# The reciprocal root of a block's variance: from GpSimd's power to Newton's steps on VectorE

## The chip, the cores and the metric

The kernel runs on one core of one Trainium2 chip. The metric is the device time of one execution in microseconds, as the median of repeated runs. The engines go by the profile's names: PE is TensorE, DVE is VectorE, ACT is ScalarE, POOL is GpSimd, SP is SyncE.

## The reference

x has 8 batches of 4096 rows by 256 values, adj is 4096 by 4096 and sparse, W is 256 by 256, all in float32. With A = relu((adj + adj^T) / 2), D the row sums of A and r = D^-0.5:

```
L   = I - diag(r) A diag(r)
out = relu(L @ (x @ W))            # for each batch
y   = (x + out - mean) / sqrt(var + 1e-5)   # over the 256 values of a row
```

The last line is what the change is about: each row of each batch needs the reciprocal square root of its variance.

## The kernel before

**First stage (up to about 600 us).** The adjacency is loaded in 512 by 512 tiles, symmetrised on TensorE and VectorE, and written to a scratch matrix a_dram. x @ W is formed, scaled by r and written to a scratch matrix g_dram, in which one row holds all 8 batches of a node (2048 values, 8 KB).

**Second stage.** The 4096 output rows are 32 blocks of 128. Block 0 is finished from products made in the first stage. The other 31 are worked off in 16 pairs u, block 2u + 1 and block 2u + 2, in the order SEQ = 1 to 7, 0, 8 to 15. For each pair an index list names the source nodes that have an entry in the pair's rows, sorted by which 64-row halves they touch. The list is cut into tiles of 128 nodes, 302 over all pairs (29 in pair 0, 24 in pair 1, 16 to 22 in the others, 9 in pair 15). A tile is one step:

- GpSimd issues two indirect DMAs: `ga` (L707), the tile's 128 rows of a_dram, and `g` (L718), its 128 rows of g_dram, up to 1 MB. The `g` tiles lie in a ring of 13 buffers. Gather n + 13 is issued in the program behind the products of tile n, whose slot it takes.
- TensorE multiplies (L905): 4 column pieces of 512 for each block that the tile touches. Products that touch only half a block (64 rows) run two at a time.

When a block has its last product, `finish` runs: ScalarE evicts four PSUM banks to `y` (`evict`, L608), VectorE adds the residual `xr` (L619) and makes the moments (L624, L626), L627 adds EPS to the variance, and `normalise` makes the power -0.5 on GpSimd (L632), subtracts the mean and multiplies on VectorE (L634, 8 instructions, one a batch), and stores the block from SyncE's queue (L642). There are four buffers for `xr`, whose loads go out on ScalarE's queue (L602), and one for `y`. The last block, 31, has a way of its own (`finish_last`): its additions and powers are on GpSimd, its scaling on ScalarE.

**The lists.** While a pair runs, VectorE and TensorE make the lists of later pairs. `prepare` puts the spreading of the list of the pair two places ahead (`spread`, L274 to L290) and the patterns of the pair four places ahead (L184 to L199) on VectorE. `lists`, after the first block of a pair is finished, puts the counting on TensorE (L209, L210, L241, L242, L295); it needs the results of L199 and L290. Its results lie in two PSUM banks that VectorE reads (L307, L308, L169 to L174), and the index steps follow (L311 to L265, L222 to L236). The gathers two pairs on read `ai` and `gi`, which come out of this.

**What sets the order.** Each engine has one queue that is worked off in order, and the code writes that order out. `queue(engine)` sets an instruction behind the last one traced on that engine. `after(n, fn)` calls a function once n further counts of products have been traced, a half block counting 1 and a whole block 2 per tile:

```
            def rest():
                z = xr.pop(i)
                with queue("dve"):
                    mv, rstd = moments(i, y, z, stat)

                def end():
                    in_turn(normalise, i, z, mv, rstd)

                after(6, end)

            after(1, rest)
```

A pair has 26 to 59 counts (10 in pair 15). GpSimd's power is part of `normalise` and so stands in GpSimd's queue between the gathers traced before and after that point; since a gather is traced 13 tiles ahead of its products, the gathers in front of a power belong to tiles up to 13 further on. A branch that computes everything densely stands at the end for inputs that the lists don't hold; it is not taken here.

Of the kernel before, what the change touches and what calls it, by code (L numbers as in the profile page):

```python
# [9 lines left out]
F32 = mybir.dt.float32  # L10
AF = mybir.ActivationFunctionType
ALU = mybir.AluOpType
AX = mybir.AxisListType
BF16 = mybir.dt.bfloat16
I32 = mybir.dt.int32
# [29 lines left out]
def kernel(  # L45
# [25 lines left out]
    nc = tc.nc  # L71
    B, N, F = x.shape
    FO = w.shape[1]
    P = 128
# [26 lines left out]
    neg_half = const.tile([P, NB], F32, name="neg_half")  # L101
# [58 lines left out]
    def blocks(u):  # L160

        return min(2, NB - 1 - 2 * u)
# [442 lines left out]
    def evict(i, py, ypool):  # L605
        y = ypool.tile([P, B, FO], F32, tag="y", name=f"y_{i}", bufs=1)
        for c in range(G // S):
            nc.scalar.activation(  # L608
                y.rearrange("p b o -> p (b o)")[:, c * S : (c + 1) * S],
                py[c],  # L610
                AF.Relu,
                scale=minus_r[:, i : i + 1],
            )
        return y

    def moments(i, y, z, stat, tag="", adder=nc.vector):

        n = z.shape[1]
        adder.tensor_add(z, z, y)  # L619
        stats = stat.tile([P, n, 6], F32, tag=f"stats{n}", name=f"stats_{i}{tag}")  # L620
        mv = stat.tile([P, n, 2], F32, tag=f"mv{n}", name=f"mv_{i}{tag}")
        rstd = stat.tile([P, n], F32, tag=f"rstd{n}", name=f"rstd_{i}{tag}")
        for b in range(n):
            nc.vector.bn_stats(stats[:, b, :], z[:, b, :])  # L624
        for b in range(n):
            nc.vector.bn_aggr(mv[:, b, :], stats[:, b, :])  # L626
        nc.vector.tensor_scalar(rstd, mv[:, :, 1], EPS, None, ALU.add)  # L627
        return mv, rstd

    def normalise(i, z, mv, rstd):  # L630
        n = z.shape[1]
        nc.gpsimd.tensor_tensor(rstd, rstd, neg_half[:, :n], ALU.pow)  # L632
        for b in range(n):
            nc.vector.tensor_scalar(  # L634
                z[:, b, :],
                z[:, b, :],
                mv[:, b, 0:1],
                rstd[:, b : b + 1],
                ALU.subtract,
                ALU.mult,  # L640
            )
        nc.sync.dma_start(out[:, i * P : (i + 1) * P, :].rearrange("b p f -> p b f"), z)  # L642
# [4 lines left out]
    def targets(u, kind):  # L647

        if kind == 0:
            kind = 15 if blocks(u) == 2 else 3  # L650
        out = []
        for b in range(2):
            h = kind >> 2 * b & 3
            if h:
                out.append((b, {1: slice(0, Q), 2: slice(Q, P), 3: slice(0, P)}[h]))
        return out
# [15 lines left out]
    with (  # L672
# [9 lines left out]
        stat = gath.enter_context(tc.tile_pool(name="stat", bufs=3))  # L682
# [10 lines left out]
        def queue(engine):  # L693

            traced = reversed(nc.cur_bb.bb.instructions)
            return tc.issue_after(next(i for i in traced if i.engine == engines[engine]))
# [34 lines left out]
        def after(n, fn, *args):  # L731
            later.append((n, fn, args))

        def run_later(by):
            ready = [l for l in later if l[0] <= by]
            later[:] = [(n - by, fn, args) for n, fn, args in later if n > by]
            for _, fn, args in ready:
                fn(*args)
# [4 lines left out]
        n = RING  # L743
# [30 lines left out]
        def finish(i):  # L774

            if i == NB - 1:
                finish_last(i)
                return
            with queue("act"):
                y = evict(i, py.pop(i), ypool)  # L780

            def rest():
                z = xr.pop(i)
                with queue("dve"):
                    mv, rstd = moments(i, y, z, stat)

                def end():
                    in_turn(normalise, i, z, mv, rstd)

                after(6, end)  # L790

            after(1, rest)

# [66 lines left out]
        def in_turn(fn, *args):  # L860

            with queue("dve"):
                fn(*args)
# [4 lines left out]
        for q, (u, step) in enumerate(steps):  # L868
            new = q == 0 or steps[q - 1][0] != u
            last = q + 1 == len(steps) or steps[q + 1][0] != u  # L870
            if new:
                after(11, prepare, u)
                after(10 if u != SEQ[-1] else 4, residuals, range(2 * u + 1, 2 * u + 1 + blocks(u)))
                left = {}
                for v, st in steps[q:]:
                    if v == u:
                        for k, t in st:
                            for b, _ in targets(u, k):
                                left[b] = left.get(b, 0) + 1
                begun = set()  # L880
                for b in range(blocks(u)):
                    py[2 * u + 1 + b] = []
            work = [(b, rows, *got[u, t]) for m in range(2) for k, t in step for b, rows in targets(u, k)[m : m + 1]]
            if work[0][1] == side != slice(0, P):
                work.reverse()
            side = work[-1][1]
            for b in sorted({wk[0] for wk in work}):
                if not py[2 * u + 1 + b]:
                    py[2 * u + 1 + b] = [
                        psum.tile([P, S], F32, tag=f"b{b}", name=f"py_{u}_{b}_{c}") for c in range(G // S)  # L890
                    ]
            fresh = []
            for b, rows, at, gt in work:
                hs = {(b, h) for h in range(2) if rows.start <= h * Q < rows.stop}
                assert not hs & begun or hs <= begun
                fresh.append(not hs & begun)
                begun |= hs
                left[b] -= 1
            for c in range(G // S):
                for (b, rows, at, gt), new_rows in zip(work, fresh):  # L900
                    both = any(len(targets(u, k)) == 2 for k, t in step)
                    off = b * P if both else 0

                    with queue("pe"):
                        last_product = nc.tensor.matmul(  # L905
                            py[2 * u + 1 + b][c][rows, :],
                            lhsT=at[:, off + rows.start : off + rows.stop],
                            rhs=gt[:, c * S : (c + 1) * S],
                            start=new_rows,
                            stop=left[b] == 0,  # L910
                            skip_group_check=True,
                        ).ins
            for k, t in step:
                gather(n)
                n += 1
            run_later(sum(1 + (rows == slice(0, P)) for _, rows, _, _ in work))
            for b in {wk[0] for wk in work}:
                if left[b] == 0:
                    finish(2 * u + 1 + b)
                    if b == 0:  # L920
                        after(2, lists, u)
# [9 lines left out]
    with tc.If(short > 0):  # L931
        with (
            tc.tile_pool(name="full", bufs=3) as full,
            tc.tile_pool(name="ypool3", bufs=2) as ypool,
            tc.tile_pool(name="stat3", bufs=3) as stat,
        ):
            for i in range(NB):
                lt = full.tile([P, NB, P], F32, tag="l", name=f"l_{i}", bufs=2)
                nc.sync.dma_start(
                    lt, a_dram[:N, i * P : (i + 1) * P].rearrange("(m p) q -> p m q", p=P)  # L940
                )
                py = [psum.tile([P, S], F32, tag="b0", name=f"pz_{i}_{c}") for c in range(G // S)]
                for m in range(NB):
                    gt = full.tile([P, G], F32, tag="g", name=f"gf_{i}_{m}", bufs=4)
                    nc.sync.dma_start(gt, g_dram[m * P : (m + 1) * P, :])
                    for c in range(G // S):
                        nc.tensor.matmul(
                            py[c],
                            lhsT=lt[:, m, :],
                            rhs=gt[:, c * S : (c + 1) * S],  # L950
                            start=(m == 0),
                            stop=(m == NB - 1),
                        )
                y = evict(i, py, ypool)
                z, _ = residual(i, ypool)
                mv, rstd = moments(i, y, z, stat)
                normalise(i, z, mv, rstd)


# [26 lines left out]
```

## Time and profile before

| | |
|---|---|
| median of 14 runs | 1627.08 us (1622.49 to 1629.72) |
| the profiled execution | 1628.85 us, span 1627.1 us |
| TensorE busy | 1496.9 us, 92% |
| VectorE busy | 828.8 us, 51% |
| GpSimd busy | 795.0 us, 49% |
| ScalarE busy | 372.5 us, 23% |
| moved by DMA | 575.69 MB, mean 354 GB/s |
| mean granted TensorE clock | 0.965 |

A line of the groups of instructions reads: line, engine, operation, what it writes <- what it reads, shapes, count | busy time in us, mean of one in ns | idle time of that engine just before these instructions and what ended most of it. A line of the waits reads: who <- for whom: us in total, how many times, the longest. A line of the timeline reads: start, length, engine, line, operation, and in brackets the idle time before it with what ended it. A line of the stretches reads: from:to, length, busy time (and instructions) of PE, PEld (weight load), DVE, ACT and POOL, the granted clock, the mean busy share of the 16 DMA engines, and GB/s. GpSimd's busy time in a gather is the making of its descriptors; the transfer comes after it.

### The profile page before, as it was taken

The numbers are of one execution on the slowest core, as the hardware profiler recorded it, in microseconds if no ns is written. First come the engines' busy times: TensorE is split into PE (matmuls) and PEld (weight loads), VectorE is DVE, ScalarE is ACT, GpSimd is POOL, SyncE is SP. The second block draws the span as 40 slices with busy tenths as digits, with TensorE's granted clock in tenths as the row PEclk, the third lists the DMA queues.
The fourth block names the chain that finished last, engine by engine and source line by source line (L and its number), as shares of the span: only waits on it lengthen the run. The fifth ranks groups of instructions, "written<-read, shape, count | busy, mean of one in ns | idle before, by whom it ended". The sixth has DMA issues, their size and how long they took to land.

```text
span 1627.1 us, 18626 instructions
## 1 busy us (share of the span) xinstructions
PE 1496.9 (92%) x6544; PEld 779.6 (48%) x6544; DVE 828.8 (51%) x1878; ACT 372.5 (23%) x462; POOL 795.0 (49%) x1120
## 2 busy tenths in 40 slices
PE   6999989998879898999999999779999899899893
PEld 5787877776666643333333333223333333333331
DVE  5675678876445604253543726445054734743543
ACT  3555554544334510101001001000001001010111
POOL 3011010101011157676777767676477777667773
PEclk9999999999989999999999999989999999999997
DMA  9999999999778889999999999899698999999995
GB/s 339 371 367 404 389 370 374 400 395 341 265 290 290 346 352 406 396 400 358 404 369 369 375 345 385 326 381 373 227 332 332 347 387 364 347 371 368 340 360 194
DMA packets 229715, 575.69 MB, mean 354 GB/s; under 512 B 20403, under 2 KB 119011, under 8 KB 191875
## 3 DMA queue, kind: packets, MB, share of 16 engines
q0 software_dynamic: 56672, 305.70, 49.0%
q1 hardware_dynamic: 100912, 134.23, 23.5%
q10 hardware_dynamic: 72032, 134.51, 22.1%
q8 instruction: 54, 0.88, 0.2%
q14 instruction: 45, 0.37, 0.1%
HBM read 479.07 MB, written 136.34 MB: 378 GB/s over the span
## 4 chain that ended last, share of the span: by engine, by line
PE 61%; DVE 13%; DMA 12%; issue 7%; POOL 4%; ACT 2%; POOLq 0%; SPq 0%; ACTq 0%; DVEq 0%; another core or an unknown queue 0%
PE py L905 40%; PE pg L457 9%; PE lead L420 5%; PE tr L360 4%; DMA a_dram<-sym 3%; PE xtr L446 3%; DMA xin<-in_x_dram 3%; DVE sym L364 2%; DMA g<-g_dram,gi 2%; DVE xr L634 2%; POOL g L718 2%; POOL ga L707 1%; DVE hot L274 1%; DMA ga<-a_dram,ai 1%; DMA adj<-in_adj_dram 1%
## 5 line engine op out<-in xcount | busy, mean ns | idle before, releaser
L905 PE MATMUL py<-g,ga 128*64 128x512 f32 (+1 forms) x3152 | 937.1, 603 | 18.4 <-issue 12.1
L905 PEld LDWEIGHTS py<-g,ga 128*64 128x64 f32 (+1 forms) x3152 | 338.1, 154 | 605.9 <-issue 583.2
L718 POOL DMA_INDIRECT g<-g_dram,gi x302 | 339.7, 1125 | 182.1 <-issue 89.5
L707 POOL DMA_INDIRECT ga<-a_dram,ai x302 | 327.5, 1084 | 98.6 <-issue 80.1
L608 ACT ACTIVATE y<-py,minus_r 128x512 f32<-128x512 f32 x120 | 82.0, 687 | 900.9 <-PE py L905 703.8
L634 DVE TENSOR_SCALAR xr<-xr,mv,rstd 128x256 f32<-128x256 f32 x248 | 86.7, 420 | 363.3 <-POOL rstd L632 316.8
L457 PE MATMUL pg<-w_sb,xt 128*128 128x256 f32 x1024 | 234.5, 388 | 5.3 <-ACT xt L447 5.2
L364 DVE TENSOR_TENSOR sym<-tr,adj 128x512 f32<-128x512 f32 x256 | 162.8, 681 | 125.9 <-PE tr L360 109.3
L457 PEld LDWEIGHTS pg<-w_sb,xt 128*128 128x128 f32 x1024 | 197.2, 195 | 34.4 <-ACT xt L447 6.0
L369 DVE TENSOR_REDUCE part<-sym 128x32 f32<-128x2048 f32 x64 | 145.3, 2277 | 63.7 <-ACT sym L368 63.7
L619 DVE TENSOR_TENSOR xr<-xr,y 128x2048 f32<-128x2048 f32 x31 | 71.2, 2296 | 190.7 <-ACT y L608 129.5
L415 POOL DMA_DIRECT2D strip<-a_dram x32 | 18.5, 581 | 294.6 <-PE lead L420 289.3
L360 PE MATMUL tr<-ident,adj 128*128 128x128 f32 x1024 | 137.6, 285 | 24.8 <-DVE sym L364 12.4
L368 ACT ACTIVATE sym<-sym 128x2048 f32<-128x2048 f32 x64 | 122.5, 1914 | 120.6 <-DVE sym L364 120.6
L360 PEld LDWEIGHTS tr<-ident,adj 128*128 128x128 f32 x1024 | 119.6, 146 | 53.0 <-DVE sym L364 24.4
L446 PE MATMUL xtr<-ident,xin 128*128 128x128 f32 x512 | 74.5, 292 | 22.8 <-DVE sym L364 13.6
L389 POOL TENSOR_TENSOR r<-e,neg_half 128x4 f32<-128x4 f32 x8 | 8.3, 1041 | 172.8 <-DVE e L388 172.8
L624 DVE BATCH_NORM_STATS2 stats<-xr 128x6 f32<-128x256 f32 x256 | 87.2, 411 | 7.2 <-POOL xr L619 6.1
L420 PE MATMUL lead<-gt,strip 128*128 128x512 f32 x176 | 82.5, 593 | 0.0
L447 ACT COPY xt<-xtr 128x512 f32<-128x512 f32 x128 | 69.0, 590 | 50.4 <-PE xtr L446 49.0
L446 PEld LDWEIGHTS xtr<-ident,xin 128*128 128x128 f32 x512 | 60.9, 149 | 39.9 <-DVE sym L364 23.8
L467 ACT ACTIVATE gt<-pg,r 128x512 f32<-128x512 f32 x88 | 60.5, 687 | 79.3 <-PE pg L457 72.0
(108 smaller groups left out, 609.6 us busy)
## 6 DMA issues: line engine op xcount, KB each, us to landing
adj<-in_adj_dram SPq DMA_DIRECT2D x64, 1024.0 KB
a_dram<-sym ACTq DMA_DIRECT2D x64, 1024.0 KB
xin<-in_x_dram SPq DMA_DIRECT2D x64, 512.0 KB
xr<-in_x_dram ACTq DMA_DIRECT2D x32, 1024.0 KB
out_dram<-xr SPq DMA_DIRECT2D x31, 1024.0 KB
g_dram<-gt ACTq DMA_DIRECT2D x22, 1024.0 KB
g_dram<-held ACTq DMA_DIRECT2D x10, 1024.0 KB
ga<-a_dram,ai POOLq DMA_INDIRECT x302
```

What stands on the lines that cost most here:

```text
L360: ins = nc.tensor.transpose(pt[:, c * P : (c + 1) * P], tji[:, c, a * P : (a + 1) * P], ident)
L364: nc.vector.tensor_add(sym[:, a, :], pt, tij[:, a, :])
L368: nc.scalar.activation(sym, sym, AF.Relu, scale=0.5)
L369: nc.vector.tensor_reduce(part[:, i * A : (i + 1) * A, j * S // Q : (j + 1) * S // Q], sym.rearrange("p a (c q) -> p a c q", q=Q), AX.X, A ...
L420: nc.tensor.matmul(lead[c], lhsT=strip, rhs=g[:, c * S : (c + 1) * S], start=not done, stop=len(done) == NB - 1, skip_group_check=True,)
L446: nc.tensor.transpose(pt[:, k, c, :], xin[b // H][:, b % H + k, c * P : (c + 1) * P], ident)
L457: ins = nc.tensor.matmul(pg[:, k * FO : (k + 1) * FO], lhsT=xt[:, b + k, c, :], rhs=w_sb[:, c, :], start=(c == 0), stop=(c == FC - 1),)
L624: nc.vector.bn_stats(stats[:, b, :], z[:, b, :])
L634: nc.vector.tensor_scalar(z[:, b, :], z[:, b, :], mv[:, b, 0:1], rstd[:, b : b + 1], ALU.subtract, ALU.mult,)
L707: nc.gpsimd.indirect_dma_start(out=at if both else at[:, :P], out_offset=None, in_=a_pairs if both else a_rows, in_offset=bass.IndirectOff ...
L718: nc.gpsimd.indirect_dma_start(out=gt, out_offset=None, in_=g_dram, in_offset=bass.IndirectOffsetOnAxis(ap=gi[:, t : t + 1], axis=0), boun ...
L905: last_product = nc.tensor.matmul(py[2 * u + 1 + b][c][rows, :], lhsT=at[:, off + rows.start : off + rows.stop], rhs=gt[:, c * S : (c + 1) ...
```

## The change

The root is made on VectorE. The bits of v = variance + EPS are taken as an integer and shifted right by one, turned into a float, and subtracted from a constant; the result, taken as float bits, is a first guess of v^-0.5. Three of Newton's steps follow. These are 12 instructions on 128 x 8 values, each needing the one before. They are called right behind `moments`, in VectorE's queue. `normalise` has no instruction on GpSimd any more and is called 3 counts later instead of 6. `prepare` is called 6 counts into a pair instead of 11. `finish_last` keeps its four powers and four additions on GpSimd, behind the last gather.

```diff
+    def inverse_root(i, v, stat):
+
+        n = v.shape[1]
+        half = stat.tile([P, n], F32, tag="half", name=f"half_{i}")
+        bits = stat.tile([P, n], I32, tag="bits", name=f"bits_{i}")
+        root = stat.tile([P, n], F32, tag="root", name=f"root_{i}")
+
+        nc.vector.tensor_single_scalar(bits, v.bitcast(I32), 1, ALU.arith_shift_right)
+        nc.vector.tensor_copy(half, bits)
+        nc.vector.tensor_scalar(root.bitcast(I32), half, -1.0, float(0x5F3759DF), ALU.mult, ALU.add)
+        for _ in range(3):
+            nc.vector.tensor_mul(half, root, root)
+            nc.vector.scalar_tensor_tensor(half, half, -0.5, v, ALU.mult, ALU.mult)
+            nc.vector.scalar_tensor_tensor(root, half, 1.5, root, ALU.add, ALU.mult)
+        return root
+
     def normalise(i, z, mv, rstd):
-        n = z.shape[1]
-        nc.gpsimd.tensor_tensor(rstd, rstd, neg_half[:, :n], ALU.pow)
-        for b in range(n):
+        for b in range(B):
...
                 with queue("dve"):
-                    mv, rstd = moments(i, y, z, stat)
+                    mv, var = moments(i, y, z, stat)
+                with queue("dve"):
+                    rstd = inverse_root(i, var, stat)
 
                 def end():
                     in_turn(normalise, i, z, mv, rstd)
 
-                after(6, end)
+                after(3, end)
...
-                after(11, prepare, u)
+                after(6, prepare, u)
...
-                mv, rstd = moments(i, y, z, stat)
-                normalise(i, z, mv, rstd)
+                mv, var = moments(i, y, z, stat)
+                normalise(i, z, mv, inverse_root(i, var, stat))
```

## The prediction

> **What bounds the kernel now.** I read the page first, then the waits of the second stage (from 581 us on, where the gathers start), then the timeline around the longest wait of TensorE, and last the stretches. On the page TensorE is busy for 1496.9 of 1627.1 us, so what can be won is small and lies in its gaps. The page's group of VectorE's normalising step shows the odd thing:
>
> ```profile
> L634 DVE TENSOR_SCALAR xr<-xr,mv,rstd 128x256 f32<-128x256 f32 x248 | 86.7, 420 | 363.3 <-POOL rstd L632 316.8
> ```
>
> VectorE stands idle for 363.3 us ahead of this line, for GpSimd's power (L632). The waits of the second stage say who pays for that:
>
> ```profile
> DVE xr L634 <- POOL rstd L632: 313.1, 28, 32.6
> PE lists L209 <- DVE kind L199: 29.8, 4, 15.1
> POOL rstd L632 <- DVE rstd L627: 20.8, 6, 5.5
> PE lists L295 <- DVE val L290: 7.2, 2, 6.1
> PE py L905 <- DMA g<-g_dram,gi: 4.9, 3, 2.5
> ```
>
> TensorE waits 29.8 + 7.2 = 37.0 us for VectorE's index lists, and only 4.9 us for a gather. The timeline of the worst case shows the chain, and how tight the gathers are beside it:
>
> ```profile
> 1002.30 0.17 DVE L627 TENSOR_SCALAR rstd<-mv 128x8 f32<-128x8 f32 x1
> ...
> 1035.08 1.02 POOL L718 DMA_INDIRECT g<-g_dram,gi  x1 [0.63 <-DMA g<-g_dram,gi]
> 1036.12 1.67 POOL L632 TENSOR_TENSOR rstd<-rstd,neg_half 128x8 f32<-128x8 f32 x1
> 1037.83 2.86 DVE L634 TENSOR_SCALAR xr<-xr,mv,rstd 128x256 f32<-128x256 f32 x8 [32.57 <-POOL rstd L632]
> ...
> 1064.11 0.47 PE L209 MATMUL lists<-kind,ones 128*128 128x352 bf16 x1 [15.07 <-DVE kind L199]
> ...
> 1065.17 1.95 POOL L718 DMA_INDIRECT g<-g_dram,gi  x1 [0.30 <-issue]
> ```
>
> The variance is ready at 1002.5. The power stands in GpSimd's queue behind gathers that are themselves late, and runs at 1036.12. VectorE waits 32.57 us, then works almost without a pause up to the lists, and TensorE, which needs them, waits 15.07 us. The stretches (us, busy time by engine, clock, DMA share, GB/s; the last two for the product tiles alone) say what lies behind that:
>
> ```profile
> 581.00:1077.00 496.00, 471.43 (x1849) 174.95 (x1849) 220.34 (x616) 38.72 (x57) 359.92 (x319) 0.99 0.98 373
> 1077.00:1195.00 118.00, 114.18 (x372) 43.07 (x370) 32.45 (x92) 6.18 (x9) 69.59 (x66) 0.97 0.85 314
> 1195.00:1590.00 395.00, 372.28 (x1432) 139.38 (x1430) 198.16 (x583) 39.86 (x59) 285.69 (x249) 0.97 0.97 358
> 640.00:740.00 100.00, 100.00 (x373) 38.46 (x373) 38.89 (x103) 6.91 (x11) 71.59 (x64) 1.00 1.02 400
> 1092.00:1102.00 10.00, 7.24 (x11) 2.27 (x12) 0.00 (x0) 0.66 1.02 400
> 1102.00:1126.00 24.00, 24.00 (x64) 9.19 (x63) 0.00 (x0) 1.00 1.03 402
> ```
>
> The DMA engines are nearly full throughout (0.97 to 0.98). Only from 1077 to 1195, where pair 0 has most products per gather, is TensorE clearly the slower side. At the end the gathers decide:
>
> ```profile
> 1589.45 1.00 POOL L718 DMA_INDIRECT g<-g_dram,gi  x1 [0.39 <-issue]
> 1595.54 5.35 PE L905 MATMUL py<-g,ga 128*64 128x512 f32 x16 [2.54 <-DMA g<-g_dram,gi]
> 1602.64 3.62 PE L905 MATMUL py<-g,ga 128*64 128x512 f32 x14 [1.75 <-DMA g<-g_dram,gi]
> ```
>
> So two chains run side by side: products with their lists, and the supply of gathers. The change touches both.
>
> **Removed.** 31 powers leave GpSimd. In the trace they cost 51.8 us of work and 21.5 us of idle queue ahead of them, 73.3 us, mostly between gathers. The 363.3 us of VectorE's idle time go with them.
>
> **Added.** 12 dependent instructions a block on 8 columns. The nearest rows are the small index steps:
>
> ```profile
> 903.28 0.17 DVE L252 SCALAR_TENSOR_TENSOR fits<-pos_r,rest 128x32 f32<-128x32 f32 x1
> ...
> 904.14 1.01 POOL L718 DMA_INDIRECT g<-g_dram,gi  x1 [0.30 <-issue]
> ...
> 904.82 0.31 DVE L265 CAST at<-digit 128x32 f32<-128x32 int32 x1
> ```
>
> L252 to L265 are eight dependent steps, and seven starts take 904.82 - 903.28 = 1.54 us, 0.22 us each. Twelve make 2.6 us a block and 82 us for 31. VectorE is busy some 467 of the 1047 us from 581 to 1628, and would be busy 549: no bound. Where GpSimd was free, the power took 1.9 us from variance to normalising, so a block's own chain gets 0.7 us longer. That is covered by the spare time below; if it were not, it would cost 31 x 0.7 = 22 us at most.
>
> **Moved.** Normalising is set 3 counts after the root instead of 6, list building (L274 to L199) 6 counts into a pair instead of 11, and in the order of the built program list building now stands ahead of the previous block's normalising. Normalising issues the store on SyncE's queue, so stores start earlier and the four residual buffers come free earlier; they add no bytes. No queue gets a new wait: the gathers keep their order on GpSimd and their waits for ring slots. What is newly queued behind the root is the reading of the lists (L307 on), which frees two PSUM banks that the next pair's products need. In pair 4 that reading starts at 875.25 after 1.93 us of waiting for TensorE, ends at 878.1, and the next pair starts at 881.8: a root of 2.6 us fills the wait, moves the end by 0.7 us and leaves 3 us to spare, so I cost it at nothing.
>
> **Where TensorE's 37.0 us go.** In the worst case the wait of 32.6 us disappears and two roots cost 5.3, so the lists come 27 us earlier against a wait of 15.1. The other three long ones (6 to 7 us, near 1294, 1417 and 1524) each follow a VectorE wait of 19.9 to 25.3 us. The earlier list building comes on top. All 37.0 should go. Slow products that follow a wait go too: in 1092 to 1102 eleven product passes ran at a clock of 0.66, which at the next stretch's 64 in 24 us are worth 4.1 us, so 6 us were lost there. All that TensorE can give back is 37.0, about 12 for such slow stretches (6 here, as much again near 1327 and right after the waits), 4.9 for gathers and 5 in the tail: 59 us.
>
> **What is late next: gathers.** Pair 0 starts at 1077, and its first gathers are issued only at 1058.45, 1062.51 and 1065.17; at the end a gather is used 11 to 13 us after its issue when TensorE waits for it. With an unchanged supply pair 0 could start only some 4 us earlier. The supply itself gains from an emptier queue, but no more than the DMA engines have left: 0.98 to 1.02 over 496 us is 19 us. I take half, 8 to 9, since part of that idle time is start-up and full ring. With the 6 us of slow clock, 4 + 9 + 6 = 19 us by 1195; the bounds are 4 and 27 (waits of 3 and 15.1, rows of slow products 9). From 1195 to 1590 the supply sets the pace. GpSimd's row for that window:
>
> ```profile
> L632 POOL TENSOR_TENSOR rstd<-rstd,neg_half 128x8 f32<-128x8 f32 x14 | 23.4, 1671 | 18.3 <-DVE rstd L627 18.0
> ```
>
> A queue that alone set the pace would give back 23.4 + 18.3 = 41.7 us. The DMA engines allow less: a share of 0.97 filled up to 1.00 gives 12 us, to 1.02 19 us. I take 15, with bounds 6 and 32, the latter being what is left of TensorE's 59. In the tail, block 30's power at 1610.03 and its normalising up to 1614.3 stand before the last block's statistics; ahead of time they free 4 us (0 to 5).
>
> **The sum.** 19 + 15 + 4 = 38 us. The profiled execution took 1628.85 us for a span of 1627.1, and lies 1.8 us above the median of 1627.08. 1628.85 - 38 = 1591, from the median 1589; I say 1590. The bounds are 11 us (1617) and 59 us (1568).
>
> **A rule that speaks against it.** GpSimd's gather at 1065.17 took 1.95 us instead of 1.00 under VectorE's large addition, while the one at 904.14 took 1.01 us in the midst of the small chain. I take the second row, no cost. The Trainium skill, SBUF — State Buffer, section Who interferes with whom, says that a VectorE instruction with two SBUF inputs contends with a GpSimd instruction that reads SBUF, and that copies and tensor_scalar in a 2-port mode block GpSimd outright. By it all 12 steps could hold up gathers, and in place of the 38 us won the sum would come near the loss of rival 3.
>
> **Rivals.**
> 1. *The DMA engines are as full as they get.* For it: shares of 0.97 to 0.98 and 20 us stretches at 1.0 with only 370 to 380 GB/s. Against it: 400 GB/s from 640 to 740. Then only 4 + 6 and a little of the tail is won: 1612 to 1617.
> 2. *TensorE sets the pace alone,* the queue was the limit: up to 59 us, 1568 to 1576. Against it: the waits for gathers at the end.
> 3. *Slower: the roots hold up the gathers.* If each root stopped descriptor making for its 2.64 us, GpSimd would lose 82 us and gain 73.3; the gathers, and with them the end, come 8.5 us later, 1636. It decides from 2.36 us a block on. The row at 904.14 speaks against it.
> 4. *No change:* lists or stores are held by something that the power's wait hid, and the end stays at 1627.
>
> **Chances.** The forecast (1577 to 1606) 0.62, rival 1 0.14, rival 2 0.12, rival 3 0.07, no change 0.05. Within 0.2% (3.3 us) is about what a measurement here cannot tell from no change. Faster 0.88, same 0.05, slower 0.07. The range 1568 to 1617 leaves out the last two cases and the edges of the first.
>
> **What would show it.** Right: no wait of VectorE at normalising, no wait of TensorE at L209 or L295 above 1 us, no clock row below 0.9 between 700 and 1500, twelve small VectorE rows near 0.2 us, gathers of 1.0 us as before, a DMA share of 1.0 from 1195 on, and more TensorE waits for gathers than 4.9 us. Wrong: gathers that take clearly longer under the roots, lists still late, or a DMA share that stays at 0.97 while the gathers are no faster.

## The result and the profile after

The changed kernel took 1608.41 us (median of 10 runs, 1600.28 to 1612.74) beside 1627.37 us for the kernel before: a ratio of 0.9889, 95% interval 0.9873 to 0.9904. In three later sets of runs it was 0.9883 (0.9855 to 0.9911), 0.9909 (0.9876 to 0.9941) and 0.9918 (0.9892 to 0.9944). So it is faster, by 11 to 20 us (the medians of each set), and not by the 37 that were forecast. The profiled execution has a span of 1610.9 us against 1627.1.

The group of VectorE's normalising step, from the page of the changed kernel (what was L634 is L648 now):

```profile
L648 DVE TENSOR_SCALAR xr<-xr,mv,root 128x256 f32<-128x256 f32 x248 | 83.9, 409 | 0.1
```

The idle time ahead of it fell from 363.3 to 0.1 us. The waits from 581 us on (L732 and L721 are the two gathers, L718 and L707 before; L921 are the products, L905 before), first two of the kernel before, then the changed kernel:

```profile
POOL g L718 <- PE py L905: 54.3, 47, 4.6
...
POOL g L718 <- DMA g<-g_dram,gi: 29.1, 30, 1.9
```

```profile
DVE xr L619 <- ACT y L608: 383.6, 19, 72.5
...
POOL g L732 <- PE py L921: 71.7, 54, 4.6
POOL g L732 <- DMA g<-g_dram,gi: 60.0, 53, 2.3
...
POOL g L732 <- DMA ga<-a_dram,ai: 25.2, 21, 2.6
...
PE py L921 <- DMA g<-g_dram,gi: 17.7, 15, 3.2
...
PEld L209 <- DVE xr L619: 2.4, 3, 0.8
```

Three things are to be seen. TensorE's waits for lists (37.0 us before) are gone; of what is left at L209 and L295 the largest is a weight load's 2.4 us. In their place stand 17.7 us of waits for gathers, all of them behind pair 0. VectorE's idle time has not gone but moved: it now waits 383.6 us for ScalarE to evict the next block (129.5 before). And GpSimd, which got rid of 73.3 us of powers and of waiting for their data, now waits longer ahead of its gathers: 60.0 us for an earlier `g` to land (29.1 before), 25.2 for an earlier `ga` (none before), 71.7 put down to products (54.3 before). That is 73.5 us more: the queue's freed time became waiting.

The list step in pair 7 on TensorE, from the timeline, where the kernel before stood still for 15.07 us; now no wait stands in front of it:

```profile
1059.84 1.88 PE L921 MATMUL py<-g,ga 128*128 128x512 f32 x4
1061.55 0.31 PE L209 MATMUL lists<-kind,ones 128*128 128x352 bf16 x1
```

And the stretches of the changed kernel, cut at the start and the end of pair 0 as they are now:

```profile
581.00:1073.00 492.00, 481.18 (x1848) 176.57 (x1848) 250.45 (x802) 39.71 (x59) 333.10 (x305) 0.99 0.98 374
1073.00:1182.00 109.00, 109.00 (x372) 41.97 (x370) 34.92 (x110) 5.18 (x9) 66.35 (x66) 1.00 0.94 347
1182.00:1580.00 398.00, 376.79 (x1432) 141.81 (x1430) 236.54 (x788) 38.60 (x58) 259.14 (x235) 0.99 0.97 362
```

The DMA share was 0.98, 0.85 and 0.97 before; it is 0.98, 0.94 and 0.97. It rose only in pair 0, where TensorE had wasted time. By the starts of products in the two traces, the 16.2 us of span split up like this:

| part | before | after | won |
|---|---|---|---|
| start of pair 0 | 1077.0 | 1073.1 | 3.9 |
| from there to the start of pair 8 | 118.8 | 109.3 | 9.5 |
| from pair 8 to the end of the last product | 410.4 | 413.7 | -3.3 |
| the tail after it | 20.9 | 14.8 | 6.1 |

Behind pair 0, in a quarter of the span and with 19.1 of TensorE's 37.0 us of list waits, nothing was won.

### The profile page after: what moved, and what is told of

The parts are those of the page before. It is cut to its first block, busy times and chain, and to the rows that moved or that the text cites. A ratio compares the mean times of both kernels' runs of the same rounds, so it can differ in the third digit from the quotient of the medians.

```text
span 1610.9 us, 18973 instructions
## 1 busy us (share of the span) xinstructions
PE 1505.6 (93%) x6544; PEld 781.8 (49%) x6544; DVE 890.7 (55%) x2250; ACT 371.9 (23%) x462; POOL 735.7 (46%) x1089
## 4 chain that ended last, share of the span: by engine, by line
PE 65%; DMA 17%; DVE 8%; issue 5%; POOL 2%; ACT 2%; SPq 0%; POOLq 0%; ACTq 0%; DVEq 0%; another core or an unknown queue 0%
PE py L921 43%; DMA g<-g_dram,gi 10%; PE pg L457 10%; PE lead L420 5%; PE tr L360 3%; PE xtr L446 3%; DVE sym L364 3%; DMA a_dram<-sym 3%; DMA xin<-in_x_dram 2%; DMA adj<-in_adj_dram 1%; DVE part L369 1%; POOL ga L721 1%; ACT sym L368 1%; DMA xr<-in_x_dram 1%; POOL g L732 1%
## 5 line engine op out<-in xcount | busy, mean ns | idle before, releaser
L921 PE MATMUL py<-g,ga 128*64 128x512 f32 (+1 forms) x3152 | 949.0, 601 | 36.0 <-DMA g<-g_dram,gi 17.7
L921 PEld LDWEIGHTS py<-g,ga 128*64 128x64 f32 (+1 forms) x3152 | 341.8, 153 | 631.7 <-issue 601.0
L732 POOL DMA_INDIRECT g<-g_dram,gi x302 | 342.0, 1132 | 248.7 <-issue 81.4
L721 POOL DMA_INDIRECT ga<-a_dram,ai x302 | 317.7, 1052 | 100.4 <-issue 84.7
L619 DVE TENSOR_TENSOR xr<-xr,y 128x2048 f32<-128x2048 f32 x31 | 71.2, 2297 | 452.9 <-ACT y L608 383.6
L446 PE MATMUL xtr<-ident,xin 128*128 128x128 f32 x512 | 73.7, 290 | 23.6 <-DVE sym L364 14.7
L648 DVE TENSOR_SCALAR xr<-xr,mv,root 128x256 f32<-128x256 f32 x248 | 83.9, 409 | 0.1
```

Source lines behind the costliest of these rows:

```text
L446: nc.tensor.transpose(pt[:, k, c, :], xin[b // H][:, b % H + k, c * P : (c + 1) * P], ident)
L648: nc.vector.tensor_scalar(z[:, b, :], z[:, b, :], mv[:, b, 0:1], rstd[:, b : b + 1], ALU.subtract, ALU.mult,)
L721: nc.gpsimd.indirect_dma_start(out=at if both else at[:, :P], out_offset=None, in_=a_pairs if both else a_rows, in_offset=bass.IndirectOff ...
L732: nc.gpsimd.indirect_dma_start(out=gt, out_offset=None, in_=g_dram, in_offset=bass.IndirectOffsetOnAxis(ap=gi[:, t : t + 1], axis=0), boun ...
L921: last_product = nc.tensor.matmul(py[2 * u + 1 + b][c][rows, :], lhsT=at[:, off + rows.start : off + rows.stop], rhs=gt[:, c * S : (c + 1) ...
```

## The experiments

The theory that the first four runs put to the test: transfers set the pace of the gathers, so only the list wait ahead of pair 0 and the tail cost time. Rival A gives the gain to the earlier list building, rival B to every list wait and every power alike. The median of the kernel before differed from one set of runs to another (1616 to 1629 us), so each kernel is read by its ratio to the runs of before beside it. "The stretch" is always the time from pair 8's first product to the end of the last product.

**The root alone.** Diff against the changed kernel:

```diff
-                after(3, end)
+                after(6, end)
...
-                after(6, prepare, u)
+                after(11, prepare, u)
```

> The root is made on VectorE as after the change, but the two delays of before stay (normalising 6 counts after the root, list building 11 counts into a pair). Theory (the DMA engines set the pace of the gathers; only the list wait ahead of pair 0 and the tail cost time): the list wait is gone already with the root alone, so about 1609 us, 1605 to 1613. Rival A (earlier list building is what wins): no more than half of the 18 us, 1617 to 1627.

Measured: 1603.46 us beside 1616.06, ratio 0.9914 (0.989 to 0.9938). That is 13 to 14 us, more than the half of the 18 that rival A allowed. The forecast in us was meant from 1627 and can't be read from 1616.

**The delays alone**, the power still on GpSimd (the same two lines of the change, made in the kernel before).

> The power stays on GpSimd as before, only the two delays of the change are made (3 counts and 6 counts). Theory: normalising still waits for GpSimd, but list building now stands ahead of the previous block's normalising and misses most of the wait: the 13 us ahead of pair 0 mostly won, the tail's 6 not, 1612 to 1620 us. Rival A as in the first run: the power is the whole cause, and normalising that is queued earlier waits longer: 1624 to 1632.

Measured: 1613.40 us, ratio 0.9979 (0.9963 to 0.9996). The time lies in the range, but that range was meant from 1627 us; beside 1616 only 3.4 us were won, not most of 13. The waits of this run from 581 us on tell more than the time:

```profile
DVE xr L634 <- POOL rstd L632: 374.1, 17, 33.0
...
PE py L905 <- DMA g<-g_dram,gi: 36.8, 21, 3.8
...
PE lists L209 <- DVE kind L199: 5.8, 2, 4.8
```

Normalising waits for GpSimd as long as ever, yet the lists hardly wait any more, since their building now stands ahead of it. TensorE got 28 of its 37.0 us of list waits back (5.8 and 3.1 are left) and waits 36.8 us for gathers. So getting rid of most of these waits was by itself worth little. The waits for gathers alone don't tell why: the root alone, in the same set, has 35.6 us of them and is 10 us faster. By the starts of products, the run with the delays alone begins pair 0 5.5 us later than the root alone, gains 3.1 in pair 0, and loses 5.1 in the stretch (415.6) and 4.6 in the tail (20.3).

**The change in one half of the pairs.** The early half:

```diff
-                with queue("dve"):
-                    rstd = inverse_root(i, var, stat)
+                if i <= 16:
+                    with queue("dve"):
+                        rstd = inverse_root(i, var, stat)
...
+                    after(3, end)
+                else:
+                    def end():
+                        in_turn(normalise_power, i, z, mv, var)
+
+                    after(6, end)
...
-                after(6, prepare, u)
+                after(6 if u <= 7 else 11, prepare, u)
```

> The change (root and delays) for the blocks up to 16 and the list building of pairs 1 to 7 and 0 alone; later blocks have the power on GpSimd and the old delays. Theory (only the list wait ahead of pair 0, and the tail, cost time; later list waits are hidden behind the gathers): 13 of the 18 us are won, 1614 us (1611 to 1617). Rival B (every list wait and every power in the queue costs): about half is won, 1618 us or more.

The late half (`i > 16`, `u > 7`):

> The reverse: root and delays of the change only from block 17 and pair 8 on; the earlier blocks as before. Theory: the tail alone is won, 4 to 6 us: 1621 to 1623 us. Rival B: half of the 18 us or more, 1618 us or less.

Measured: early 0.9955 (0.9938 to 0.9971), 7 us; late 0.996 (0.9944 to 0.9976), 6.5 us. By the ratios it looks like rival B's even split, but the traces say where the late half's share lies: its stretch takes 409.5 us and its tail 14.7, where the early half's stretch takes 413.5 and its tail 20.8. These are TensorE's waits in the stretch, first in the early half's run, whose stretch is built as before, then in the late half's:

```profile
PE lists L209 <- DVE kind L199: 23.4, 3, 13.3
...
PE lists L295 <- DVE val L290: 6.5, 1, 6.5
...
PE py L932 <- DMA g<-g_dram,gi: 4.5, 2, 2.5
```

```profile
PE py L932 <- DMA g<-g_dram,gi: 23.7, 20, 2.6
```

29.9 us of list waits went, 19 us of waits for gathers came, and the stretch is 4 us shorter, but it also began 10 us later. Beside the 410.4 us of the kernel before, the late half wins the tail and next to nothing else. The early half began pair 0 at 1062.8 instead of the 1076.1 of the late half's run, lost 3 of these 13.3 us in pair 0 and 4 more in the stretch; so the theory's 13 us were won at that place and half of them did not last.

**The whole change again, and fewer bytes.** The next runs test what holds the stretch. The changed kernel as it is:

> The changed kernel itself, beside the next three on one chip. Both theories: 0.987 to 0.991 of before. In its profile the stretch from the start of pair 8 to the last product takes 409 to 414 us, as in every profile so far, with the change or without.

Measured: 1609.01 us beside 1629.49, ratio 0.9883 (0.9855 to 0.9911); the stretch takes 414.3 us. The same with a quarter of the stores left out:

```diff
-        nc.sync.dma_start(out[:, i * P : (i + 1) * P, :].rearrange("b p f -> p b f"), z)
+        nc.sync.dma_start(out[:6, i * P : (i + 1) * P, :].rearrange("b p f -> p b f"), z[:, :6])
```

> The changed kernel that stores only 6 of the 8 batches of every block but the last (the output of two batches is left out): 8.1 MB less for the DMA engines, some 22 us of their time at 366 GB/s, half of it behind pair 0; TensorE, VectorE and GpSimd have the same work. Theory (the DMA engines set the pace behind pair 0): the time falls by 12 to 20 us against the changed kernel, 8 to 11 of them between pair 8 and the last product. Rival C (waits of gathers for one another, or TensorE, set it): 0 to 5 us.

> The same cut of the stores in the kernel before (two batches of the output left out). Theory: also limited by the DMA engines behind pair 0, so 8 to 16 us less than before; ahead of pair 0 the list wait stays and eats most of that half. Rival C': the kernel before is limited by the list waits and powers in the queue and not by transfers: 0 to 4 us.

Measured: 0.9845 (0.9816 to 0.9874) for the changed kernel, 6 us less than whole, and 0.9926 (0.9903 to 0.9949) for the kernel before, 12 us less. The stretch falls from 414.3 to 402.3 us, and in the kernel before to 406.1 from the 410.4 of its first profile. In the stretch the theory's 8 to 11 us are there, though the profile is of the fastest of the five runs; by the medians, of runs that scatter by 12 us, the changed kernel's 6 us lie near the rival's end. So a larger cut was made: 2 of 8 batches stored (`out[:2`, `z[:, :2]`).

**The changed kernel a third time, and with few stores:**

> The changed kernel once more, as the measure for the next three on one chip: 0.986 to 0.991 of before.

> The changed kernel that stores only 2 of the 8 batches of every block but the last (the output of six batches is left out): 24.4 MB less, some 67 us of the DMA engines' time, 32 of them behind pair 0. Theory (transfers set the pace behind pair 0 until TensorE does): the stretch from pair 8 to the last product falls from 413 to 384 to 392 us, which is what it holds without TensorE's waits; the time falls by 20 to 32 us. Rival C (not the bytes, but gathers waiting for one another, four in flight): no further than with 8.1 MB less, the stretch stays at 400 us or above and the time falls by 4 to 12 us.

Measured: 1611.13 us (ratio 0.9909, 0.9876 to 0.9941) and 1571.17 us (0.9673, 0.9643 to 0.9702), 40 us apart, more than expected. The stretch falls from 412.3 to 385.0 us, as the theory said, with TensorE busy 365.4 of 370:

```profile
1166.00:1536.00 370.00, 365.38 (x1428) 138.49 (x1426) 231.65 (x768) 38.21 (x57) 262.12 (x234) 0.99 0.96 357
```

What I had not counted is that the pairs ahead of pair 0 are held by transfers too: pair 0 starts at 1055.5 instead of 1072.9. Nothing on TensorE, VectorE or GpSimd was changed here; leaving out bytes gave 40 us. The share is 0.96 and the rate 357 GB/s, almost as with all stores (0.97 and 362), though TensorE now hardly waits. Shorter stores also free the residual buffers sooner; no run parts the two.

**The change with few stores.** If list waits and transfers run side by side and the later one counts, the change must be worth more once transfers are few. Both sides of it, first in different sets of runs and then side by side (the measure for the first set was the changed kernel once more):

> The changed kernel, as the measure for the next three on one chip: 0.986 to 0.992 of before.

Measured: 1605.11 us beside 1615.86, 0.9918 (0.9892 to 0.9944).

> The kernel before with stores of 2 of 8 batches for every block but the last (the output of six batches is left out), to be set against the changed kernel with the same cut (0.9673 of before). Theory (list waits and transfers run side by side, and the later one sets the time): with fewer transfers the list waits that the change removes decide, so the change is worth more, 28 to 40 us: 0.985 to 0.992 of before, with 25 us or more of list waits in the profile. Rival E (the list waits never cost anything but ahead of pair 0): the change is worth 18 us or less here too, 0.979 or below.

> The changed kernel with stores of 2 of 8 batches for every block but the last, beside the next run on one chip: 0.966 to 0.972 of before.

> The kernel before with the same cut. Theory (waits and transfers side by side, the later one counts): 22 to 34 us slower than the run beside it, more than the change is worth with all stores. Rival E (transfers have no part in what the change is worth): 10 to 20 us slower.

Measured: the kernel before with the cut 0.9814 (0.9792 to 0.9837), which is 0.0141 or 23 us off 0.9673, between the two theories; but there the kernel before took 1615.86 us and for the 0.9673 it took 1626.41, so the two are a poor pair. Side by side: 1556.12 us (0.9624, 0.9597 to 0.965, a little lower than expected) against 1584.74 us (0.9791, 0.9766 to 0.9816), 28.6 us apart by the medians and 27 by the ratios. With all stores the change is worth 11 and 13 us by the same two measures in the set whose kernel before took 1615.86 us, much like the 1617.82 here. TensorE's waits from 581 us on, of the kernel before with the cut:

```profile
PE lists L209 <- DVE kind L199: 25.0, 4, 13.0
...
PE lists L295 <- DVE val L290: 5.6, 2, 5.0
PE py L905 <- DMA g<-g_dram,gi: 2.2, 1, 2.2
```

and the one that answers to them in the changed kernel with the cut:

```profile
PE py L921 <- DMA g<-g_dram,gi: 10.6, 7, 2.6
```

Here the list waits (30.6 us) are paid for, and taking them away brings 27 to 29 us. The stretch alone falls from 398.5 to 386.1 us, where with all stores the change won nothing in it. This shows the cause: the waits were real and could be removed, but with all stores transfers take more than half of them back (11 to 13 us are left in sets of this kind). Rival E falls.

**What the queue and the small instructions cost.** GpSimd also makes the power, into a tile that nobody reads (3 counts behind the root, where `normalise` now stands, not 6):

```diff
+        if spare is not None:
+            nc.gpsimd.tensor_tensor(spare[1], spare[0], neg_half[:, :B], ALU.pow)
```

> The changed kernel, with GpSimd also making each block's power where it stood before, into a tile that nobody reads: the queue holds what it held before, but no work waits for it. Theory (the queue has time to spare): within 4 us of the changed kernel. Rival D (the powers in the queue are what costs): 8 to 18 us slower than the changed kernel, back to before.

Measured: ratio 0.9906 (0.9873 to 0.994) beside 0.9883, 4 us by the ratios and 9 by the medians (1617.80 and 1609.01), with runs from 1604.66 to 1622.63. Between nothing and half of the gain; the 57 us of queue time (53.2 of powers, 3.4 of idle time before them) that come back are not the whole of it, and may be none of it: this profile also has the most stops of TensorE without a visible cause, 24.1 us (the last section). Then three times as many Newton steps (`range(9)` for `range(3)`):

> The changed kernel with nine Newton steps instead of three, that is 18 more small dependent VectorE instructions a block (about 3.7 us a block at 0.205 us each, 115 us in all). Theory: VectorE has the time and the small instructions don't slow the gathers: within 4 us of the changed kernel. Rival 3 of the prediction (small VectorE instructions hold up descriptor making): GpSimd loses up to 115 us in gathers, 20 us slower or more, with gathers clearly over 1.0 us.

Measured: ratio 0.9938 (0.9916 to 0.9959) beside 0.9909, 5 us more by the ratios, 6 by the medians, a little over the 4 of the theory and far from 20. The gathers of the nine steps from 581 us on, and then of the changed kernel:

```profile
L721 POOL DMA_INDIRECT ga<-a_dram,ai x301 | 329.9, 1096 | 91.7 <-issue 84.7 <-DMA g<-g_dram,gi 3.0 <-DVE stats L624 0.9
L732 POOL DMA_INDIRECT g<-g_dram,gi x301 | 329.8, 1096 | 244.8 <-issue 80.1 <-DMA g<-g_dram,gi 75.9 <-PE py L921 53.7
```

```profile
L732 POOL DMA_INDIRECT g<-g_dram,gi x302 | 342.0, 1132 | 248.7 <-issue 81.4 <-PE py L921 71.7 <-DMA g<-g_dram,gi 60.0
L721 POOL DMA_INDIRECT ga<-a_dram,ai x302 | 317.7, 1052 | 100.4 <-issue 84.7 <-DMA g_dram<-held 8.6 <-DMA g<-g_dram,gi 4.3
```

329.9 + 329.8 and 342.0 + 317.7 are both 659.7 us, for 602 gathers and for 604, so 1.096 us each instead of 1.092: the extra small instructions add next to nothing to descriptor making. The trace shows it more directly: gathers that overlap nothing but Newton's steps take 0.98 us on average (106 of them), gathers that overlap nothing on VectorE take 0.98 too (192). By what else the steps cost their 5 us no run shows.

**The root alone, beside the whole change:**

> The root alone on VectorE, with the two old delays, this time beside the whole change. Theory: the root alone has the whole gain, within 3 us of the changed kernel. Rival A: the earlier list building has its own part, 4 to 8 us slower than the changed kernel.

Measured: 0.9925 (0.9896 to 0.9954) beside 0.9909, 3 us. In the sets whose kernel before took 1616 us, 0.9914 for the root alone stands beside 0.9918 for the whole change. The root has the gain, and the delays add nothing to it that can be told from none.

**Loads spread, and a shorter ring:**

```diff
-                after(10 if u != SEQ[-1] else 4, residuals, range(2 * u + 1, 2 * u + 1 + blocks(u)))
+                after(10 if u != SEQ[-1] else 4, residuals, [2 * u + 1])
+                if blocks(u) == 2:
+                    after(24, residuals, [2 * u + 2])
```

> The changed kernel, with the second of a pair's two residual loads (1 MB each) 24 counts into the pair instead of 10, behind the first: the same bytes, less bunched. Theory (the total of the bytes counts): within 4 us of the changed kernel. Rival F (a burst of 2 MB delays the gathers that TensorE needs, and leaves the engines short of work later): 5 to 12 us faster, with fewer TensorE waits for gathers than 20 us.

> The changed kernel with a ring of 11 gather buffers instead of 13. Theory: behind pair 0 the ring is rarely full, so it costs only where TensorE is the slower side (pair 0 and the pairs at the start): two buffers fewer ahead of it, some 3 to 7 us. Rival G (the ring's depth sets the pace of the supply): 15 us or more.

Measured: loads spread 0.9938 (0.9918 to 0.9958) beside 0.9918, 1604.19 us beside 1605.11, the stretch 410.1 beside 411.5: no gain to be told from none, so rival F falls and it is not the bunching. A ring of 11 (`RING = 11`): 0.994 (0.992 to 0.996), 1606.51 us, 1 to 4 us slower; the stretch takes 416.5. The ring's depth is not what sets the pace. With all stores in place no run was faster than the changed kernel by more than the scatter between its own sets (ratios of 0.9883 to 0.9918).

## Why the prediction was wrong

The direction held, and so did most of the steps: the wait at normalising went, all 37.0 us of list waits went, the roots' instructions take 0.17 to 0.19 us each as the small index steps did, VectorE is no bound, no gather got longer. Even the list of what would show it wrong had the right case: "a DMA share that stays at 0.97 while the gathers are no faster".

The step that failed is "What is late next: gathers": it has the supply of gathers setting the pace behind pair 0, which the runs bear out, and then lets that supply grow faster because GpSimd's queue is emptier. It did not. Term by term:

- **15 us from 1195 to 1590** (share of 0.97 filled up to 1.00). Measured: -3.3 us; this is the term that failed in every set. The share is 0.97 again, and 19.1 us of list waits became 17.7 us of waits for gathers. In every profile with all stores, whichever part of the change it has, the stretch takes 409.5 to 416.5 us; only fewer bytes moved it, to 385 us with 24.4 MB less. GpSimd's row of 41.7 us, which I held for the supply's reserve, had no part in it.
- **9 us of supply gained ahead of pair 0** (0.98 to 1.02). Measured: none; pair 0 started 3.9 us earlier, the 4 us of "unchanged supply". In the set of the first four runs it started 13.3 us earlier and gave back 3.0 in pair 0 and 4.0 behind it.
- **6 us of slow products.** Measured: 9.5 us in pair 0, that is the stop-and-go around 1092 and what followed it. That this came out large is in part luck. The prediction took the slow products for a consequence of the list wait ahead of them, but a wait alone does not bring them: the late half's run waits 13.00 us at the same L209 and then has no stop in pair 0, which takes 109.3 us. Such stops come in one kind of sets of runs and not in the other (the last section). In the profiles here they sum to 12.1 us before and 15.1 after, in other places.

The row of the late half's run that this rests on:

```profile
1062.66 0.47 PE L209 MATMUL lists<-kind,ones 128*128 128x352 bf16 x1 [13.00 <-DVE kind L199]
```

The term for 581 to 1195 as a whole, 19, came to 13.4, and to 10.4 in the set of the first four runs. The last term:

- **4 us in the tail.** Measured: 6.1.

13.4 - 3.3 + 6.1 = 16.2 us, the difference of the spans. The mistake behind the terms of 15 and 9 is one: I took the share of one good stretch (640 to 740, 1.02 with 400 GB/s) for a level that the engines can keep up. The changed kernel has both kinds of stretch next to each other:

```profile
1230.00:1240.00 10.00, 10.00 (x48) 3.08 (x44) 9.35 (x47) 0.82 (x2) 6.59 (x8) 1.00 0.77 283
1360.00:1370.00 10.00, 10.00 (x31) 3.64 (x30) 9.52 (x33) 0.00 (x0) 8.17 (x7) 1.00 1.05 397
```

In the second, loads and stores of blocks run beside the gathers; in the first, gathers run alone. The mean of 0.97 is a mix of such stretches. What leaves the engines short in the first kind stays open. Over the whole second stage a gather now waits longer for an earlier one to land (60.0 + 25.2 us); in the order of the program its issue waits for the gather of the same kind four tiles earlier, so no more than four tiles are under way. But in the first stretch above no wait of GpSimd is put down to a landing: it makes descriptors for 6.59 of the 10 us.

Rival 1, "the DMA engines are as full as they get", came nearest, with 0.14, and its 1612 to 1617 was 4 us too high, since pair 0 itself and the tail gave 15.6 us where it counted 6 and a little. Rival 2 asked what TensorE alone would give; the run with few stores comes near it in the stretch, 385 us. Rival 3 (roots that hold up gathers) fell with the nine steps. The Trainium skill, SBUF — State Buffer, section Who interferes with whom, says that a VectorE instruction with two SBUF inputs contends with a GpSimd instruction that reads SBUF; the prediction left out that the same section tells of a probe in which `tensor_tensor` did not stall a DMA. The traces agree with neither in full: Newton's steps, most of which have two inputs, add nothing that can be measured, while the large additions do hold up gathers (the last section).

## What to carry to other kernels

Before a removed wait is booked as a gain, ask which other chain reaches the same point, and price the rest by that chain's measured pace. A busy share averages stretches of different kinds, and the best one is no level that the whole can be filled up to. Nor does the share alone say what the bound is: it was 0.97 where transfers set the pace and still 0.96 with few stores, where TensorE was busy for 365.4 of 370 us. A cheap test is to leave out bytes: here a cut of the stores took 40 us off without a change to TensorE's, VectorE's or GpSimd's work, and only then were the waits worth nearly what the profile had shown (27 to 29 us instead of 11 to 13).

## What the runs showed of the hardware

The same kernels ran in two kinds of sets of runs, on one and the same chip too. In one the kernel before takes 1616 to 1618 us and pair 1 takes 81.9 us, in the other 1626 to 1629 us and 89 to 94 us. The stretch from 610 to 630 us of the changed kernel shows the difference, first in a run of the second kind (0.9889), then in one of the first (0.9918):

```profile
610.00:630.00 20.00, 15.29 (x34) 5.08 (x32) 5.10 (x12) 0.00 (x0) 13.48 (x13) 0.83 1.03 405
```

```profile
610.00:630.00 20.00, 20.00 (x55) 7.50 (x53) 6.41 (x23) 0.00 (x0) 13.32 (x13) 1.00 1.02 401
```

TensorE makes 34 product passes instead of 55, with stops of up to 2.21 us for nothing that the profile shows and at a lower clock. Such stops come again later: from 581 us on they sum to 10.4 to 24.1 us in each of the ten profiles of the second kind, with the change or without, and none is listed ahead of products in the ten of the first. Why, no run here tells. It bears on the case: where the changed kernel starts pair 0 10 us earlier, it gets only some 5 us faster (the kernel before 11), as one expects of a kernel that transfers hold. Its waits for gathers are then 36.8 us instead of 17.7:

```profile
PE py L921 <- DMA g<-g_dram,gi: 36.8, 28, 3.6
```

Also unexpected: GpSimd's gathers are stretched by large two-input operations of VectorE (L619 and L274 here), and only by those that began first. Two rows of the changed kernel show it, an addition and a gather that began while it ran:

```profile
1225.65 2.29 DVE L619 TENSOR_TENSOR xr<-xr,y 128x2048 f32<-128x2048 f32 x1 [20.00 <-ACT y L608]
1226.48 2.34 POOL L732 DMA_INDIRECT g<-g_dram,gi  x1 [1.30 <-DMA g<-g_dram,gi]
```

The gather ends 0.88 us after the addition, and takes 2.34 us. In this trace the 33 gathers that began during such an addition (L619) take 2.26 us on average, the 16 that had begun before it 0.99. The list building's L274, 1.2 us long, does the same: 1.59 us for 32 gathers, 0.99 for 13. Gathers that overlap normalising alone (L648, also on 128 x 256 float32 values, with one tensor as input) take 0.99 us, those that overlap nothing on VectorE 0.97.
